# Query, key and value of a graph transformer by 26 block products instead of 3 x 7, with the token sums on GpSimd

## The chip, the cores and the metric

The kernel runs on one core of one Trainium2 chip. The metric is the device time of the whole kernel in microseconds, inputs and output in HBM, everything in fp32.

## What is computed

128 graphs of 128 nodes with 512 features each pass through two layers. The reference, cut to what matters here:

```python
# layer 0: x (128, 128, 512), adj (128, 128, 128), 8 heads of 64
h = relu(layernorm(x))
q, k, v = (h @ W.T + b for (W, b) in ((Wq, bq), (Wk, bk), (Wv, bv)))   # W: 512 x 512
scores = einsum('bhqd,bhkd->bhqk', q, k) * 64 ** -0.5 * (adj + adj)
x = x + (softmax(scores) @ v) @ Wo.T + bo
# layer 1
h = relu(layernorm(x))
Wh = h @ W
e = leaky_relu(Wh @ a[:512] + (Wh @ a[512:]).T)
att = softmax(where(adj > 0.5, e, -9e15), axis=1)
x = x + elu(att @ Wh)
```

The three products of `h` with Wq, Wk and Wv are what the change is about.

## The kernel before, in words

A *pair* `p` is two graphs (N = 64 pairs), a *group* `g` is two pairs: 4 graphs, 512 rows of `h`. 32 groups are worked through; Q, K and V are made a group at a time, everything else a pair or a graph at a time.

**Hidden rows.** `hAs[g]` holds the transposed `h` of a group: features on the partitions, in four blocks of 128 features by two pairs of 256 rows. The rows arrive transposed from HBM (`load_xT`). `hidden(p, 0)` (L222, VectorE) subtracts the mean and `hidden(p, 1)` (L224, VectorE) applies relu and scale; the numbers of a row come through HBM (`spread0` on GpSimd's DMA queue, `fetch0` on SyncE's).

**Products.** Each of Q, K and V is a 512 x 512 by 512 x 512 product, cut 2 x 2 by 2 x 2 in blocks of 256 and done with 7 block products instead of 8 (`PRODUCTS`, L130; Strassen's scheme in Winograd's form). One block product is `product` (L238): four matmul statements of 256 columns at L258. Its left operands need sums of row blocks: `token_sum` (L148 to L157) makes four per group on VectorE (`hidden_sum`, tile `hS`). Sums of weight blocks are made once at the start (`weight_sum`). The results gather in three PSUM accumulators for each of Q, K and V, `acc_a`, `acc_b` and `acc_c`. `acc_a` is read out while it still gathers: `first` copies its state into `qT`, `kT` or `v` on ScalarE (L270 for v, L275 with the bias), and `add` adds `acc_b` or `acc_c` on top on VectorE (L279).

**The rest of a pair.** `scores` (L320) makes `sc` per graph; VectorE weighs it with the adjacency (L327), takes maxima, ScalarE exponentiates and normalises, VectorE transposes 32 x 32 blocks, and two DMAs through HBM place them. `context` (L388) gives `pc` in PSUM; `keep_context` (L395) copies it to `cxT`. The output product with Wo and the later one with layer 1's W use the same seven-product scheme by rows: four token sums (`cs`, on `cxT`; `gs`, on `gT`), then `product_rows` (L299), whose accumulators `row_a` and `row_c` are added into `x` (L402) or copied and added into `z` (L495, L499). `shift` (L234, VectorE) adds a constant row to `x`. Layer 1's gather is L481 (`pg`), its dots L425, its ends `finish_a` and `finish_b` (L511, L515).

**PSUM.** One pool, `ps1` (L57), of eight buffers of 2 KB per partition serves every matmul output.

**The order.** The program states the order of all instructions by hand. `HEAD` (L577) lists steps with their pair, `ORDER` (L601) one repetition with a lag for each step, `TAIL` (L611) the end. `ORDER` is run once for each pair. Each engine takes its instructions from that list in order; between engines only data and buffers make them wait. In the names of steps, `U1` to `U11` are products, `F` and `A` their read-outs, `sca`, `scb` the scores of a pair's two graphs, `pca`, `pcb` their contexts, `o0` to `o6` and `w0` to `w6` the row products, `cs`, `gs` and `hs` the token sums, `hd0` and `hd1` the two halves of `hidden`, `sh` the shift, `lx`, `lT`, `l0` loads.

Of the kernel before, what the change touches and what calls it, by code (L numbers as in the profile page):

```python
# [10 lines left out]
OP = mybir.AluOpType  # L11
# [13 lines left out]
def kernel(  # L25
# [6 lines left out]
    wqT: bass.AP,  # L32
    bq: bass.AP,
    wkT: bass.AP,
    bk: bass.AP,
    wvT: bass.AP,
# [23 lines left out]
    xs, x0s, adjs, adjTs, hAs, hSs = {}, {}, {}, {}, {}, {}  # L60
# [18 lines left out]
    def half_of_hidden(p):  # L79

        g, i = divmod(p, 2)
        if g not in hAs:
            hAs[g] = grp.tile([P, 4, 2, 2 * S], F32, name="hA")
        return hAs[g][:, 2 * i : 2 * i + 2].rearrange("p q c k -> p (q c) k")
# [19 lines left out]
    def column(src, name):  # L104
# [10 lines left out]
    wv_sb, wq_sb, wk_sb, wo_sb, w1_sb = (  # L115
        const.tile([P, 7, 2, E // 2], F32, name=name) for name in ("wv", "wq", "wk", "wo", "w1")
    )
# [16 lines left out]
    FIRSTS = {0: (0, 0), 2: (1, 0), 4: (1, 1), 5: (0, 1)}  # L134
    ADDS = {1: (0, 0, "b"), 4: (1, 1, "c"), 6: (1, 0, "c")}
# [12 lines left out]
    def token_sum(h, s, k):  # L148

        if k == 0:  # L150
            nc.vector.tensor_tensor(s[:, 0], h[:, 2], h[:, 3], OP.add)
        elif k == 1:
            nc.vector.tensor_tensor(s[:, 1], s[:, 0], h[:, 0], OP.subtract)  # L153
        elif k == 2:
            nc.vector.tensor_tensor(s[:, 2], h[:, 0], h[:, 2], OP.subtract)
        else:
            nc.vector.tensor_tensor(h[:, 2], h[:, 1], s[:, 1], OP.subtract)  # L157
# [59 lines left out]
    def hidden(p, k):  # L217

        h = hAs[p // 2][:, 2 * (p % 2) : 2 * (p % 2) + 2].rearrange("p q c k -> p (q c) k")
        row = rows0[p][:, None, :, k].to_broadcast([P, 2 * 2, 2 * S])  # L220
        if k == 0:
            nc.vector.tensor_tensor(h, h, row, OP.subtract)  # L222
        else:
            nc.vector.scalar_tensor_tensor(h, h, 0.0, row, op0=OP.max, op1=OP.mult)  # L224

    def hidden_sum(g, k):
        if g not in hSs:
            hSs[g] = grp.tile([P, 3, 2, 2 * S], F32, name="hS")
        token_sum(hAs[g], hSs[g], k)

    def shift(p):


        nc.vector.tensor_tensor(xs[p], xs[p], c_sb[:, None, :].to_broadcast([P, 2, E]), OP.add)  # L234

    accs = {}

    def product(g, which, n):  # L238

        if n == 0:  # L240
            if which == "v":
                vs[g] = grp.tile([P, G, E], F32, name="v")
            else:
                qks[g, which] = {}
        if which != "v" and n in (0, 2):
            qks[g, which][n // 2] = grp.tile([P, C, 2 * S], F32, name=which + "T", bufs=3 if which == "q" else 2)
        w = {"q": wq_sb, "k": wk_sb, "v": wv_sb}[which]
        ha, wb, bank = PRODUCTS[n]
        fresh = (g, which, bank) not in accs
        if fresh:  # L250
            accs[g, which, bank] = ps1.tile([P, 2, 2 * S], F32, name="acc_" + bank, tag="ps1")
        acc = accs[g, which, bank]
        h = hAs[g][:, ha] if ha < 4 else hSs[g][:, ha - 4]
        for m in range(2):
            ms = slice(m * P, (m + 1) * P)
            for c in range(2):
                lhsT, rhs = (h[:, c, ms], w[:, wb, c, :]) if which == "v" else (w[:, wb, c, ms], h[:, c, :])
                nc.tensor.matmul(  # L258
                    acc[:, m, :], lhsT, rhs, start=fresh and m == 0 and c == 0, stop=c == 1, skip_group_check=True
                )  # L260

        def dst(t, f):
            if which == "v":
                return vs[g][:, 2 * t : 2 * t + 2, f * 2 * P : (f + 1) * 2 * P]
            return qks[g, which][t][:, 2 * f : 2 * f + 2, :]

        def first(t, f):
            a = accs[g, which, "a"]
            if which == "v":
                nc.scalar.copy(dst(t, f), a)  # L270
            else:
                bias = bk_sb if which == "k" else bq_sb
                for m in range(2):
                    j = 2 * f + m
                    nc.scalar.activation(dst(t, f)[:, m, :], a[:, m, :], AF.Identity, bias=bias[:, j : j + 1])  # L275

        def add(t, f, bank):
            d = dst(t, f)
            nc.vector.tensor_tensor(d, accs[g, which, bank], d, OP.add)  # L279

        def firsts():
            if n in FIRSTS:
                first(*FIRSTS[n])

        def adds():
            if n in ADDS:
                add(*ADDS[n])

        return firsts, adds
# [20 lines left out]
    def scores(b):  # L310
        p, i = divmod(b, 2)
        g, h = divmod(p, 2)
        qT, kT = qks[g, "q"][h], qks[g, "k"][h]
# [80 lines left out]
    def keep_context(b):  # L394
        nc.scalar.copy(rows_of(cxT, b % 2), pcs.pop(b))  # L395
# [88 lines left out]
    def keep_gathered(p, i):  # L484
        if p not in gTs:
            gTs[p] = work.tile([P, 7, 2, S], F32, name="gT")
        nc.scalar.copy(rows_of(gTs[p], i), pgs.pop((p, i)))  # L487
# [77 lines left out]
    SEQ = "v0 v1 v2 v3 v4 q0 v5 q1 v6 q2 q3 q4 k0 q5 k1 q6 k2 k3 k4 k5 k6".split()  # L565
# [6 lines left out]
    EARLY, LATE = 3, 4  # L572
# [197 lines left out]
    with tc.manual_schedule():  # L770
# [9 lines left out]
        for p in range(EARLY, N - LATE):  # L780
            for step, lag in ORDER:
                if p >= lag:
                    do(step, p - lag)
# [45 lines left out]
```

## Time and profile before

| | us |
|---|---|
| runs | 2347.01, 2351.15, 2352.15 |
| median | 2351.15 |
| profiled execution, first to last instruction | 2346.1 |
| TensorE busy in it | 2332.0 |
| TensorE weight loads | 2061.2 |
| VectorE busy | 2000.4 |
| ScalarE busy | 1467.2 |
| GpSimd busy | 257.0 |

The profile gives the profiled execution's span, from its first to its last instruction, and no separate time for it; the three runs lie 0.9 to 6.1 us above that span. The granted TensorE clock was 0.998 of full speed. Tables of groups name a line, an engine, an operation, `out<-in` by the program's tile names, the shape and the count; behind the bar stand busy time, mean ns of one, and the engine's idle time just before with what ended it. A fp32 matmul statement appears as two MATMUL records.

### The profile page before, as it was taken

How to read it: one execution, taken by the hardware profiler on the slowest of the kernel's cores; microseconds unless marked ns; L12 is line 12 of the kernel's file. 1: busy time of each engine (PE TensorE's matmuls, PEld its weight loads, DVE VectorE, ACT ScalarE, POOL GpSimd, SP SyncE). 2: the span in 40 equal slices, each digit the busy share in tenths (PEclk: the TensorE clock that was granted, in tenths of full speed). 3: DMA queues.
4: the chain of work that ended last, by engine and by line, in shares of the span. 5: the costliest groups of instructions: out<-in, count | busy, mean ns of one | idle time of the engine just before them, and what ended most of it. 6: DMA issues, size and time to landing. Idle time of an engine off the chain costs nothing.

```text
span 2346.1 us, 41028 instructions
## 1 busy us (share of the span) xinstructions
PE 2332.0 (99%) x14184; PEld 2061.2 (88%) x14184; DVE 2000.4 (85%) x4113; ACT 1467.2 (63%) x4815; POOL 257.0 (11%) x320
## 2 busy tenths in 40 slices
PE   9999999999999999999999999999999999999998
PEld 8888888888888888888888888888888888888886
DVE  6888888888888888888888888888888888888888
ACT  3656666666566665666666666656666566666774
POOL 1101101111101011011110111110101101110000
PEclk9999999999999999999999999999999999999999
DMA  5445454454444554544535445444454453453332
GB/s 171 131 113 157 121 147 120 124 164 125 143 131 119 148 139 130 143 114 142 155 122 149 120 123 165 124 144 131 120 148 137 131 145 108 146 153 116 118 120 95
DMA packets 267351, 314.06 MB, mean 134 GB/s; under 512 B 24200, under 2 KB 192136, under 8 KB 267144
## 3 DMA queue, kind: packets, MB, share of 16 engines
q1 hardware_dynamic: 263112, 311.31, 45.0%
q8 instruction: 112, 1.84, 0.3%
q0 software_dynamic: 1920, 0.13, 0.2%
q14 instruction: 95, 0.78, 0.1%
q10 hardware_dynamic: 2112, 0.01, 0.1%
HBM read 210.51 MB, written 100.85 MB: 133 GB/s over the span
## 4 chain that ended last, share of the span: by engine, by line
PE 99%; DVE 0%; ACT 0%; DMA 0%; issue 0%; POOL 0%; SPq 0%; ACTq 0%; DVEq 0%; POOLq 0%
PE acc_a L258 29%; PE row_a L299 24%; PE acc_c L258 14%; PE row_c L299 9%; PE acc_b L258 7%; PE sc L320 5%; PE pc L388 5%; PE pg L481 5%; PE pt L197 0%; DMA x<-in_x 0%; PE pm L531 0%; DVE st L165 0%; ACT z L495 0%; PE pu L553 0%; DVE z L499 0%
## 5 line engine op out<-in xcount | busy, mean ns | idle before, releaser
L339 ACT ACTIVATE at<-at,nmx 128x128 f32<-128x128 f32 x1024 | 396.3, 390 | 19.8 <-DVE nmx L334 17.9
L348 ACT ACTIVATE at<-at,rs 128x128 f32<-128x128 f32 x1024 | 325.0, 391 | 12.8 <-DVE rs L343 12.1
L299 PE MATMUL row_a<-wo,cxT 128*128 128x256 f32 x1280 | 328.5, 379 | 0.3 <-DVE cxT L153 0.3
L299 PE MATMUL row_a<-w,gT 128*128 128x256 f32 x1280 | 319.4, 380 | 2.9 <-DVE z L499 1.7
L172 POOL TENSOR_SCALAR mv<-mv 128x2 f32<-128x2 f32 x124 | 79.2, 639 | 2016.8 <-DVE mv L166 1994.6
L299 PEld LDWEIGHTS row_a<-w,gT 128*128 128x128 f32 x1280 | 242.3, 190 | 37.9 <-DVE z L499 2.6
L299 PEld LDWEIGHTS row_a<-wo,cxT 128*128 128x128 f32 x1280 | 242.6, 190 | 34.3 <-DVE cxT L153 0.6
L402 DVE TENSOR_TENSOR x<-row_a,x 128x256 f32<-128x256 f32 x320 | 135.3, 423 | 133.1 <-PE row_a L299 129.8
L495 ACT COPY z<-row_a 128x256 f32<-128x256 f32 x256 | 94.3, 368 | 203.7 <-PE row_a L299 203.6
L275 ACT ACTIVATE kT<-acc_a,bk 128x256 f32<-128x256 f32 x256 | 106.5, 466 | 168.2 <-PE acc_a L258 165.0
L327 DVE SCALAR_TENSOR_TENSOR at<-sc,adj 128x512 f32<-128x512 f32 x256 | 165.1, 686 | 42.2 <-PE sc L320 39.8
L339 ACT ACTIVATION_READ_ACCUMULATOR at<-at,nmx 128x1 f32 x1024 | 193.3, 189 | 0.0
L275 ACT ACTIVATE qT<-acc_a,bq 128x256 f32<-128x256 f32 x256 | 106.1, 466 | 123.0 <-PE acc_a L258 123.0
L165 DVE BATCH_NORM_STATS2 st<-x 128x6 f32<-128x512 f32 x256 | 176.1, 688 | 7.4 <-DMA x<-in_x 5.1
L425 DVE SCALAR_TENSOR_TENSOR junk<-h,u 128x512 f32<-128x512 f32 x256 | 173.3, 677 | 0.6
L355 DVE STREAM_TRANSPOSE tr<-at 128x1024 f32<-128x1024 f32 x128 | 158.8, 1240 | 9.2 <-PE pc L388 2.7
L334 DVE TENSOR_REDUCE nmx<-at 128x8 f32<-128x1024 f32 x128 | 156.2, 1220 | 4.3
L487 ACT COPY gT<-pg 128x512 f32<-128x512 f32 x128 | 74.6, 584 | 123.8 <-PE pg L481 117.4
L481 PEld LDWEIGHTS pg<-w,h 128*128 128x128 f32 x1024 | 133.3, 192 | 6.6 <-ACT z L495 0.2
L173 POOL TENSOR_TENSOR mv<-mv,mhalf 128x2 f32<-128x2 f32 x128 | 131.1, 1024 | 30.7 <-DVE mv L168 20.3
L481 PE MATMUL pg<-w,h 128*128 128x128 f32 x1024 | 134.1, 275 | 0.0
L299 PE MATMUL row_c<-w,gT 128*128 128x256 f32 x512 | 133.0, 382 | 0.6 <-DVE z L499 0.5
(130 smaller groups left out, 4876.4 us busy)
## 6 DMA issues: line engine op xcount, KB each, us to landing
blocks<-tr SPq DMA_DIRECT2D x128, 512.0 KB, 6.8
aT<-blocks SPq DMA_DIRECT2D x512, 128.0 KB, 2.9
x<-in_x SPq DMA_DIRECT2D x123, 512.0 KB, 5.0
out<-x SPq DMA_DIRECT2D x63, 512.0 KB, 4.1
hA<-in_xT SPq DMA_DIRECT2D x120, 256.0 KB, 3.7
mr<-rows SPq DMA_DIRECT2D x60, 256.0 KB, 4.4
adj<-in_adj SPq DMA_DIRECT2D x64, 128.0 KB, 4.3
adjT<-in_adjT SPq DMA_DIRECT2D x64, 128.0 KB, 4.2
```

What stands on the lines that cost most here:

```text
L165: nc.vector.bn_stats(st, src[:, i, :])
L258: nc.tensor.matmul(acc[:, m, :], lhsT, rhs, start=fresh and m == 0 and c == 0, stop=c == 1, skip_group_check=True)
L275: nc.scalar.activation(dst(t, f)[:, m, :], a[:, m, :], AF.Identity, bias=bias[:, j : j + 1])
L299: nc.tensor.matmul(acc, left[:, la, c, :], w[:, wb, c, :], start=n in (0, 3) and c == 0, stop=c == 1, skip_group_check=True)
L327: nc.vector.scalar_tensor_tensor(ats[b][0][:, k * C : (k + 1) * C, :], scs[b][k], QSCALE, adjs[p][:, i : i + 1, :].to_broadcast([P, C, S]) ...
L334: nc.vector.tensor_reduce(nmx, at, AX.X, OP.max, negate=True)
L339: nc.scalar.activation(at[:, j, :], at[:, j, :], AF.Exp, bias=nmx[:, j : j + 1], accum_out=sums[:, j : j + 1])
L348: nc.scalar.activation(at[:, j, :], at[:, j, :], AF.Copy, scale=rs[:, j : j + 1])
L355: nc.vector.transpose(trs[b], at.rearrange("p h (j k) -> p j h k", k=Q))
L402: nc.vector.tensor_tensor(d, row_acc(p, "o", bank), d, OP.add)
L425: nc.vector.scalar_tensor_tensor(junk, h2[:, i, :], 1.0, u_sb[:, k, :], op0=OP.mult, op1=OP.mult, accum_out=ws[:, i, 1:2] if k else src_sb ...
L481: nc.tensor.matmul(pg[:, c, :], h1s[p][0][:, i, c * P : (c + 1) * P], wts[p][:, i, :], start=True, stop=True)
```

## The change

Q, K and V are no longer three separate products of 2 x 2 blocks. The rows of a group are seen as 2 pairs of 256 rows, the features as 4 blocks of 128, the outputs as 4 blocks of 128: a 2 x 4 by 4 x 4 product of blocks, which takes 26 block products instead of 32. The same 26 left operands ("forms": blocks of `h` or sums of them) serve Q, K and V at once.

- `wT` holds the three weights side by side in 16 blocks; `w_sb` has 28 slots of 3 x 128 columns. 35 sums of weight slots (`block_sum`, VectorE) are made at the start instead of 12 larger ones (those of Wo and W stay).
- 17 sums of row blocks (`make_form`, GpSimd, 128 x 256 each, eight buffers `tf`) replace four 128 x 512 sums on VectorE.
- `product_qk` (2 statements of 256 columns) and `product_v` (2 statements of 128 columns) run each of 26 terms. Terms gather in 4 chains, each with an accumulator for Q and K and one for V; 24 terms are followed by a read-out (`take_qk`, `take_v`): the first one of each of the 8 output blocks on ScalarE, the 16 later ones as an add or a subtraction on VectorE.
- `hidden(p, 0)` and `shift` go from VectorE to GpSimd, each in halves of 512 elements.
- The token sums of `cxT` and `gT` read their unmixed blocks from PSUM (`pc`, `pg`) rather than from the copies that ScalarE makes. Those copies are still made.
- `HEAD`, `ORDER` and `TAIL` are new; one repetition of `ORDER` covers two pairs, and `pca`, `pcb`, `scb` follow each other while `sca` stands alone.

```diff
-        h = hAs[p // 2][:, 2 * (p % 2) : 2 * (p % 2) + 2].rearrange("p q c k -> p (q c) k")
-        row = rows0[p][:, None, :, k].to_broadcast([P, 2 * 2, 2 * S])
+        h = half_of_hidden(p)
+        row = rows0[p][:, None, :, k].to_broadcast([P, C, 2 * S])
         if k == 0:
-            nc.vector.tensor_tensor(h, h, row, OP.subtract)
+            for c in range(0, C, 2):
+                nc.gpsimd.tensor_tensor(h[:, c : c + 2], h[:, c : c + 2], row[:, c : c + 2], OP.subtract)
...
-        nc.vector.tensor_tensor(xs[p], xs[p], c_sb[:, None, :].to_broadcast([P, 2, E]), OP.add)
+        for i in range(2):
+            nc.gpsimd.tensor_tensor(xs[p][:, i, :], xs[p][:, i, :], c_sb, OP.add)
...
+    def make_form(g, k):
+
+        a, op, b = FORMS[k]
+        forms[g, 2 * C + k] = grp.tile([P, 2 * S], F32, name="tf", bufs=8)
+        eng = nc.gpsimd
+        eng.tensor_tensor(forms[g, 2 * C + k], form(g, a), form(g, b), OP.add if op == "+" else OP.subtract)
...
+    def product_qk(g, n):
+
+        _, f, slot, _ = TERMS[n]
+        acc, fresh = fresh_acc(g, n, "q", [P, 2, 2 * S])
+        for i in range(2):
+            nc.tensor.matmul(
+                acc[:, i, :], w_sb[:, slot, i, :], form(g, f), start=fresh and i == 0, stop=True, skip_group_check=True
+            )
+
+    def product_v(g, n):
+
+        _, f, slot, _ = TERMS[n]
+        acc, fresh = fresh_acc(g, n, "v", [P, 2, P])
+        for i in range(2):
+            nc.tensor.matmul(
+                acc[:, i, :], form(g, f)[:, i * P : (i + 1) * P], w_sb[:, slot, 2, :],
+                start=fresh and i == 0, stop=True, skip_group_check=True,
+            )
+
+    def take_qk(g, n):
+
+        chain, _, _, (t, j, sign) = TERMS[n]
+        acc = accs[g, chain, "q"]
...
+        d = qks[g, t][:, :, j, :]
+        if (g, t, j) not in begun:
+            begun.add((g, t, j))
+            for i, bias in enumerate((bq_sb, bk_sb)):
+                nc.scalar.activation(d[:, i, :], acc[:, i, :], AF.Identity, bias=bias[:, j : j + 1], scale=float(sign))
+        else:
+            nc.vector.tensor_tensor(d, d, acc, OP.add if sign > 0 else OP.subtract)
...
+        if (g, t, j, "v") not in begun:
+            begun.add((g, t, j, "v"))
+            nc.scalar.activation(d, acc, AF.Copy, scale=float(sign))
+        else:
+            nc.vector.tensor_tensor(d, d, acc, OP.add if sign > 0 else OP.subtract)
...
-            nc.vector.tensor_tensor(s[:, 0], h[:, 2], h[:, 3], OP.add)
+            nc.vector.tensor_tensor(s[:, 0], block(2), h[:, 3], OP.add)
...
-            nc.vector.tensor_tensor(s[:, 1], s[:, 0], h[:, 0], OP.subtract)
+            nc.vector.tensor_tensor(s[:, 1], s[:, 0], block(0), OP.subtract)
...
-            nc.vector.tensor_tensor(s[:, 2], h[:, 0], h[:, 2], OP.subtract)
+            nc.vector.tensor_tensor(s[:, 2], block(0), h[:, 2], OP.subtract)
...
-            nc.vector.tensor_tensor(h[:, 2], h[:, 1], s[:, 1], OP.subtract)
+            nc.vector.tensor_tensor(h[:, 2], block(1), s[:, 1], OP.subtract)
...
-    EARLY, LATE = 3, 4
+    EARLY, LATE = 2, 3
```

`block(q)` is a slice of the PSUM tile `pc` or `pg`. The terms that the prediction names are of `Q` (Q and K) and `V` (V) with their number in the list of 26, `T` with a number is a form's sum, `A` and `B` are the read-outs of `Q` and `V`. Around these read-outs the new `ORDER` reads, in two places:

```
... A6:0 Q13:0 Q8:0 V8:0 gs1:2 exa3:-1 A8:0 Q10:0 A11:0 T13:0 ...
... V18:0 ata1:-2 B19:0 V21:0 od4c:0 o6:0 e1:1 ez:2 sw:1 g0:1 ...
```

## The prediction

> **What bounds the kernel now.** I read the page's shares and chain first, then the timeline of TensorE at mid-run, then the groups by line and shape, then the waits. One "double pair" below means four graphs, the unit in which both kernels repeat; there are 32.
>
> ```profile
> PE 2332.0 (99%) x14184; PEld 2061.2 (88%) x14184; DVE 2000.4 (85%) x4113; ACT 1467.2 (63%) x4815; POOL 257.0 (11%) x320
> PE 99%; DVE 0%; ACT 0%; DMA 0%; issue 0%; POOL 0%; SPq 0%; ACTq 0%; DVEq 0%; POOLq 0%
> ```
>
> TensorE is busy for 99% of the span and holds all of the chain that ended last. Busy alone proves little where matmuls overlap, so the timeline (start, busy, engine, line, out<-in, count) is needed for start to start:
>
> ```profile
> 999.88 1.05 PE L481 MATMUL pg<-w,h 128*128 128x128 f32 x8
> 1000.77 1.89 PE L258 MATMUL acc_c<-hS,wq 128*128 128x256 f32 x8
> 1002.50 1.05 PE L481 MATMUL pg<-w,h 128*128 128x128 f32 x8
> 1003.49 2.06 PE L320 MATMUL sc<-kT,qT 64*128 64x128 f32 x32
> 1005.47 1.97 PE L388 MATMUL pc<-aT,v 128*64 128x128 f32 x32
> 1007.37 1.99 PE L258 MATMUL acc_a<-hS,wq 128*128 128x256 f32 x8
> 1009.20 1.03 PE L299 MATMUL row_a<-w,gT 128*128 128x256 f32 x4
> ...
> 1072.10 1.05 PE L481 MATMUL pg<-w,h 128*128 128x128 f32 x8
> ```
>
> There is no hole: each block starts where the next one's distance says. A matmul statement shows as two records. Eight records of 256 columns take 1002.50-1000.77 = 1.73 us, 0.216 each; eight of 128 columns take 1000.77-999.88 = 0.89, 0.111 each, with a new weight load for every one. A turn between full tiles and the half tiles of sc or pc costs about 0.1 us: pg before sc takes 0.99 and not 0.89, and the first full block after pc 1.83 and not 1.73. The same step comes back at 1072.10, so a double pair takes 72.2 us.
>
> The stretch from 100 to 800 us (PE, PEld, DVE, ACT, POOL busy) has TensorE at 100% and VectorE at 86%, which is 600.11/700 x 72.2 = 61.9 us of each double pair, 10.3 us free:
>
> ```profile
> 100.00:800.00 700.00, 700.00 (x4284) 620.13 (x4283) 600.11 (x1232) 442.90 (x1455) 79.00 (x97) 1.00 0.46 134
> ```
>
> The prices, from the groups by line and shape (busy and mean ns of one behind the bar, then idle time before them):
>
> ```profile
> L279 DVE TENSOR_TENSOR qT<-acc_c,qT 128x512 f32<-128x512 f32 x64 | 43.7, 683 | 4.8 <-PE acc_c L258 4.8
> L499 DVE TENSOR_TENSOR z<-row_c,z 128x256 f32<-128x256 f32 x128 | 53.0, 414 | 1.0 <-ACT z L495 0.8 <-PE row_c L299 0.2
> L222 DVE TENSOR_TENSOR hA<-hA,mr 128x1024 f32<-128x1024 f32 x60 | 72.9, 1216 | 0.0
> L234 DVE TENSOR_TENSOR x<-x,c 128x1024 f32<-128x1024 f32 x64 | 78.2, 1221 | 53.7 <-DMA x<-in_x 53.6
> L172 POOL TENSOR_SCALAR mv<-mv 128x2 f32<-128x2 f32 x124 | 79.2, 639 | 2016.8 <-DVE mv L166 1994.6
> ```
>
> ```profile
> 21.11 0.68 DVE L153 TENSOR_TENSOR hS<-hS,hA 128x512 f32<-128x512 f32 x1
> 21.72 0.68 DVE L155 TENSOR_TENSOR hS<-hA 128x512 f32<-128x512 f32 x1
> ```
>
> The second fence is VectorE's timeline at the start. Two operations of 0.68 start 0.61 apart, so each occupies the engine some 0.07 us less than its duration. VectorE's own waits, from the list of waits, are mostly for TensorE:
>
> ```profile
> DVE x L402 <- PE row_a L299: 129.8, 137, 2.0
> DVE at L327 <- PE sc L320: 39.8, 60, 1.2
> ```
>
> That is 169.6/32 = 5.3 us per double pair which VectorE can afford today.
>
> **What the Trainium skill says.** "TensorE: Matmul & The Clock Gate", Back-to-back issue gap, gives 134 cycles for 128 columns and 262 for 256, but warns that with a weight load per matmul the spacing at 128 columns grows. The trace's 0.111 against 0.216 shows the halving and no weight-load limit. "GPSIMD Engine Reference", 3.1, gives 4497 ns for a two-input fp32 add of 2048 elements and says that the engine is about half as fast as VectorE; nothing in this trace shows such an add. "SBUF — State Buffer", Who interferes with whom, says that a VectorE instruction with two SBUF inputs and a GpSimd instruction that reads SBUF lock each other out for a whole instruction; the trace before has no GpSimd work on which to see it.
>
> **The change, part by part.**
>
> *Products.* Removed: 3 x 7 products of 4 statements, 168 records of 256 columns, 168 x 0.216 = 36.3 us per double pair. Added: 26 terms with 2 statements of 256 columns (Q, K) and 2 of 128 (V): 104 x 0.216 + 104 x 0.1115 = 22.5 + 11.6 = 34.1. Gain 2.2 us on the path. At worst a V block of four pays a little more than a pg block of eight; if each of 26 lost 0.03 us, that is 0.8 back. I take 0.
>
> *Turns.* The new order runs scb behind pca and pcb, but sca alone among full tiles. Per pair that makes five turns and two returns to full tiles where there were three turns and one return: 7 x 0.095 against 4 x 0.095, +0.28 per pair, +0.57 per double pair. Net TensorE: -1.65, so 70.55 us if nothing makes it wait. Over 32: -53 us.
>
> *VectorE.* Removed per double pair: four sums hS and hA (4 x 0.685 = 2.74), nine adds of L279 (6.13), L222 twice (2.43), L234 twice (2.44): 13.74 us in 17 instructions. Added: of 26 terms 24 are read out, 8 of them first (ScalarE) and 16 later, each later one as a 128x512 add for Q and K (0.683, like L279) and a 128x256 add for V (0.415, like L499): 10.93 + 6.64 = 17.57 us in 32 instructions. Net +3.83, less 15 x 0.07 of overlap: +2.8. Busy 64.7 of 70.55, 92%, 5.9 free where 10.3 were. The token sums of cxT and gT read PSUM instead of SBUF; L402 and L499 read PSUM at 0.41-0.42 and the SBUF sums take 0.40-0.42, so 0. They no longer wait for ScalarE's copy (0.7 us in all today), but pc and pg stay in their PSUM buffers until VectorE is done.
>
> *ScalarE.* 16 Q and K evictions stay 16 at 0.466; four V copies of 512 (0.583) become eight of 256 (0.368): +0.6 us on an engine at 63%. Off the path: nothing.
>
> *GpSimd.* Added: 17 sums of 256 elements, four halves of the subtraction and four of the shift at 512. By the skill's 2.2 ns an element (an estimate) 17 x 0.56 + 8 x 1.12 = 18.5 us; with L172's 0.64 us for two elements as a fixed cost on each of the 25, 34.5. With the 8.1 us it has (79.00/700 x 72.2) it is 27 to 43 us of 70: not a bound by load. But row statistics (L172, L173) now queue behind sums, and behind a subtraction that waits for its DMA. Most sums are issued 5 to 69 us of TensorE work ahead of their first product; T16, T12 and T6 only 1.8, 3.1 and 5.2.
>
> *The lock.* 18 VectorE instructions per double pair have two SBUF inputs (scaling of hidden 2, dots 8, the finish 4, mask and shares 4). If GpSimd reads for 18.5 of 70.55 us (26%) and a hit waits half an instruction, 0.4 us, that is 18 x 0.26 x 0.4 = 1.9 us. From below 0 (no lock), from above 5 (the long GpSimd durations). I take 2: VectorE 66.7 of 70.55, 95%.
>
> *Waits that are left.* A term's next product into the same accumulator waits for the read-out of the one before. In the new order Q10 stands 0.45 us of TensorE work behind Q8, whose read-out is two ScalarE instructions of 0.47, and V21 1.3 us behind V19 with 1.5 us of VectorE work queued between. Others have 1.7 to 20 us. With 3.9 us free on VectorE and 5.3 us of its waits to fit in, I take 0.5 us of new TensorE waits per double pair: +16 us. Lower bound 0; the upper one is rival 1.
>
> *Start and end.* 35 sums of weight blocks (128x384, about 0.49 us each, between L499's and L279's cost) stand where 12 of 0.61 stood: 17.2 - 7.3 = +10 us of VectorE before the products run freely. The first Q product needs a sum of the second pair's hidden rows, the first one now needs the first pair's alone and starts at 11.4 us. Part of this was idle TensorE already: +6, between 0 and 15. The end keeps its steps: 0. SP issues 4 weight DMAs where 6 were: nothing.
>
> *Sum.* 2346.1 - 53 + 6 + 16 = 2315 us of span. The median of the runs shown lies 5 us above the span: 2320.
>
> **Rivals.**
> 1. *VectorE becomes the bound: slower.* Its 64.7 us, 2.8 us of lock, and waits for TensorE as long as today's 5.3 make 72.8; with 0.2 for read-outs held up behind the statistics, 73.0. Over 32 that is +0.8 x 32 = 26, start +6: 2346 + 32 + 5 = 2383. It decides once lock plus waits exceed 72.2 - 64.7 = 7.5 us. For it: the sum of today's waits and the lock is within half a microsecond of that. Against: most of today's waits are spare time of an engine at 86% and shrink as it fills.
> 2. *The gain is eaten by latency.* GpSimd sums arriving late (three of them with under 5.3 us in hand) or PSUM: four chains hold two accumulators each, four of eight buffers at any time, and pc and pg hold theirs longer. Waits of 1.4 us per double pair: 2346 - 53 + 6 + 45 + 5 = 2349, no change. Against: GpSimd at 27-43 of 70 us has room.
> 3. *No new wait and no dearer start.* 2346 - 53 + 5 = 2298. Against: today's evenness rests on 10 us of free VectorE.
>
> **How the numbers follow.** Forecast 0.62 (2298 to 2340), rival 1 0.20, rival 2 0.13, rival 3 0.05. About 0.2% either way, 2346 to 2356, is what a measurement can tell from no change. Rival 2 straddles it: 0.04 below, 0.06 in, 0.03 above. So faster 0.71, same 0.06, slower 0.23. The range 2290 to 2378 leaves out half of rival 1 and little below.
>
> **What would show it.** Right: blocks of 128-column acc_v at 0.11 us a record, a double pair of 70.5 to 71.5 us, TensorE at 98%, VectorE near 94%. Rival 1: VectorE above 96% and TensorE waiting for its acc_q and acc_v adds in steady state; two-SBUF-input groups (L425's 677 ns and the finish's 1.2 us) grown by 10% or more. Rival 2: TensorE waiting for tf sums, or for buffers of pc and pg. The start is wrong if the first 60 us hold over 20 us of idle TensorE. A GpSimd sum of 256 elements over 1.3 us would break the load sum.

## The result, and the profile after

| us | before | after |
|---|---|---|
| median of the runs | 2351.64 (2347.01 to 2352.15) | 2471.76 (2470.09 to 2476.72) |
| span of the profiled execution | 2346.1 | 2470.0 |
| TensorE busy | 2332.0 | 2334.7 |
| VectorE busy | 2000.4 | 2175.2 |
| GpSimd busy | 257.0 | 987.1 |
| one double pair, mean over the middle of the run | 72.2 | 75.76 |

The change makes the kernel slower: the ratio of the medians is 1.052, with a 95% interval of 1.050 to 1.053. The forecast of 2320 is missed by 152 us and lies on the other side of the kernel before. (The median of before is now of four runs; the table ahead of the prediction had three.)

The page of after, shares and chain:

```profile
PE 2334.7 (95%) x15464; PEld 2038.7 (83%) x15464; DVE 2175.2 (88%) x4620; ACT 1470.0 (60%) x4943; POOL 987.1 (40%) x1112
PE 72%; DVE 14%; DMA 7%; issue 3%; SPq 2%; ACT 2%; POOL 0%; DVEq 0%; POOLq 0%; ACTq 0%
```

No engine is full. TensorE holds 72% of the chain where it held 99%, and the rest is VectorE and transfers. GpSimd, the engine with the new work, has no part in it. The stretch from 100 to 800 us (columns as before) says how much TensorE lacks:

```profile
100.00:800.00 700.00, 670.67 (x4483) 587.57 (x4483) 623.88 (x1336) 424.83 (x1440) 289.12 (x327) 1.00 0.44 127
```

A TensorE that shows as busy is not always at work: 670.67/700 x 75.76 = 72.6 us busy per double pair stand for 70.9 us of blocks (worked out below, step by step). The timeline of TensorE shows such a lack, and that its own prices are as forecast:

```profile
1038.19 1.03 PE L297 MATMUL acc_q<-hA,w 128*128 128x256 f32 x4
1039.05 1.03 PE L346 MATMUL row_a<-wo,cxT 128*128 128x256 f32 x4
1039.92 0.61 PE L306 MATMUL acc_v<-w,hA 128*128 128x128 f32 x4
1040.36 1.03 PE L297 MATMUL acc_q<-hA,w 128*128 128x256 f32 x4
1042.89 0.68 PE L306 MATMUL acc_v<-w,tf 128*128 128x128 f32 x4 [1.50 <-ACT v L334]
1043.41 1.03 PE L346 MATMUL row_c<-wo,cxT 128*128 128x256 f32 x4
```

Four records of 256 columns take 1039.92-1039.05 = 0.87 us, four of 128 columns 1040.36-1039.92 = 0.44. Then `V6` starts 2.53 us behind its predecessor, which needed 0.87: 1.7 us are lost to a ScalarE copy of `v` (`B4`). Why the copy was late is in VectorE's timeline of the same moment, of which these lines count (behind the bracket, idle time and what ended it), and in ScalarE's:

```profile
1037.08 0.42 DVE L449 TENSOR_TENSOR x<-row_a,x 128x256 f32<-128x256 f32 x1
1040.12 0.42 DVE L449 TENSOR_TENSOR x<-row_a,x 128x256 f32<-128x256 f32 x1 [2.61 <-PE row_a L346]
1040.46 0.68 DVE L205 BATCH_NORM_STATS2 st<-x 128x6 f32<-128x512 f32 x1
...
1041.59 0.17 DVE L390 RECIPROCAL rs<-sums 128x4 f32<-128x4 f32 x1
```

```profile
1041.79 0.69 ACT L395 ACTIVATE at<-at,rs 128x128 f32<-128x128 f32 x2 [2.08 <-DVE rs L390]
1042.39 0.36 ACT L334 ACTIVATE v<-acc_v 128x256 f32<-128x256 f32 x1
```

VectorE stands 2.61 us at `od1`, an addition of `row_a` into `x` (L449), whose tile `row_a` TensorE is still writing. Behind `od1` in VectorE's fixed queue stands, after some other work, a reciprocal of 0.17 us; for it ScalarE stands 2.08 us; behind that in ScalarE's queue stands the copy; for it TensorE stands. A wait of VectorE for TensorE has come back to TensorE through two queues.

The chain in order of time (start, us, what) shows the other end of the same wait:

```profile
1039.22 0.88 PE row_a L346 x4
...
1040.46 0.70 DVE st L205
...
1045.32 1.16 DVE tr L402
1046.50 3.97 DMA blocks<-tr
...
1053.77 1.16 DVE nmr L459
...
1060.39 1.65 DVE junk L472 x2
1062.03 0.35 DVE gT L197
1062.52 1.10 PE row_a L346 x4
```

From 1040 to 1062 us VectorE works with a single pause of 0.16 us, and at the end TensorE waits for a token sum. That this is what had piled up behind the wait is a reading of the chain. The groups by line and shape give the prices (columns as before):

```profile
L323 DVE TENSOR_TENSOR qk<-qk,acc_q 128x512 f32<-128x512 f32 x512 | 335.1, 671 | 7.2 <-PE acc_q L297 4.4
L336 DVE TENSOR_TENSOR v<-v,acc_v 128x256 f32<-128x256 f32 x512 | 208.2, 408 | 40.3 <-PE acc_v L306 37.4
L282 POOL TENSOR_TENSOR tf<-hA,tf 128x256 f32<-128x256 f32 x288 | 259.4, 905 | 386.4 <-PE acc_v L306 260.6 <-PE acc_q L297 124.6
L472 DVE SCALAR_TENSOR_TENSOR junk<-h,u 128x512 f32<-128x512 f32 x256 | 229.5, 896 | 6.3 <-ACT h L465 2.7
L263 POOL TENSOR_TENSOR hA<-hA,mr 128x512 f32<-128x512 f32 x120 | 191.7, 1617 | 70.3 <-DMA hA<-in_xT 59.5 <-PE sc L367 6.7 <-issue 2.5
L459 DVE SCALAR_TENSOR_TENSOR nmr<-mv 128x2 f32<-128x2 f32 x64 | 38.9, 608 | 0.2 <-POOL mv L213 0.2
```

The read-outs cost what was forecast (0.683 and 0.415 were taken). The dots have grown from 677 to 896 ns, and an operation of two columns (L459) from 155 to 608. The list of waits (us in all, times, longest):

```profile
ACT at L386 <- DVE nmx L381: 198.2, 118, 5.4
DVE x L449 <- PE row_a L346: 149.6, 94, 2.6
ACT at L395 <- DVE rs L390: 78.0, 63, 3.3
PEld acc_v L306 <- POOL tf L282: 41.9, 23, 1.9
PE acc_v L306 <- ACT v L334: 41.2, 28, 1.5
PE acc_q L297 <- ACT qk L321: 16.5, 34, 0.9
```

In the kernel before ScalarE waited 17.9 us in the place of the first line and 12.1 in that of the third. VectorE's wait for `row_a` hasn't shrunk with VectorE's free time: 149.6 us now, 129.8 before. The fourth line, weight loads for V that wait for a GpSimd sum, looks like rival 2, but belongs to the copy of the line below it: the sum that `V6` reads, `T5`, is made a repetition earlier (`T5:-2`), and in e2_dead below, where nobody waits for GpSimd, the same loads wait 57.2 us for the copy.

### The profile page after: what moved, and what is told of

It is laid out like the page before. It is cut to its first block, busy times and chain, and to the rows that moved or that the text cites. A ratio compares the mean times of both kernels' runs of the same rounds, so it can differ in the third digit from the quotient of the medians.

```text
span 2470.0 us, 45694 instructions
## 1 busy us (share of the span) xinstructions
PE 2334.7 (95%) x15464; PEld 2038.7 (83%) x15464; DVE 2175.2 (88%) x4620; ACT 1470.0 (60%) x4943; POOL 987.1 (40%) x1112
## 4 chain that ended last, share of the span: by engine, by line
PE 72%; DVE 14%; DMA 7%; issue 3%; SPq 2%; ACT 2%; POOL 0%; DVEq 0%; POOLq 0%; ACTq 0%
PE acc_q L297 20%; PE row_a L346 18%; PE acc_v L306 12%; PE row_c L346 8%; PE sc L367 5%; PE pc L435 4%; DMA aT<-blocks 4%; PE pg L528 4%; DVE junk L472 3%; SPq L412 2%; DMA blocks<-tr 2%; DVE qk L323 1%; DVE hA L265 1%; DVE st L205 1%; DVE x L449 1%
## 5 line engine op out<-in xcount | busy, mean ns | idle before, releaser
L297 PE MATMUL acc_q<-tf,w 128*128 128x256 f32 x2176 | 556.3, 383 | 17.7 <-ACT qk L321 15.9
L297 PEld LDWEIGHTS acc_q<-tf,w 128*128 128x128 f32 x2176 | 393.1, 190 | 76.7 <-ACT qk L321 23.3
L282 POOL TENSOR_TENSOR tf<-hA,tf 128x256 f32<-128x256 f32 x288 | 259.4, 905 | 386.4 <-PE acc_v L306 260.6
L306 PEld LDWEIGHTS acc_v<-w,tf 128*128 128x128 f32 x2176 | 312.3, 191 | 89.4 <-POOL tf L282 41.9
L306 PE MATMUL acc_v<-w,tf 128*128 128x128 f32 x2176 | 334.0, 279 | 42.9 <-ACT v L334 40.5
L323 DVE TENSOR_TENSOR qk<-qk,acc_q 128x512 f32<-128x512 f32 x512 | 335.1, 671 | 7.2 <-PE acc_q L297 4.4
L297 PE MATMUL acc_q<-hA,w 128*128 128x256 f32 x1152 | 291.0, 380 | 0.8 <-ACT qk L321 0.6
L449 DVE TENSOR_TENSOR x<-row_a,x 128x256 f32<-128x256 f32 x320 | 134.1, 419 | 151.0 <-PE row_a L346 149.6
L336 DVE TENSOR_TENSOR v<-v,acc_v 128x256 f32<-128x256 f32 x512 | 208.2, 408 | 40.3 <-PE acc_v L306 37.4
L297 PEld LDWEIGHTS acc_q<-hA,w 128*128 128x128 f32 x1152 | 211.2, 190 | 26.5 <-ACT qk L321 1.3
L263 POOL TENSOR_TENSOR hA<-hA,mr 128x512 f32<-128x512 f32 x120 | 191.7, 1617 | 70.3 <-DMA hA<-in_xT 59.5
```

Source lines behind the costliest of these rows:

```text
L263: nc.gpsimd.tensor_tensor(h[:, c : c + 2], h[:, c : c + 2], row[:, c : c + 2], OP.subtract)
L282: eng.tensor_tensor(forms[g, 2 * C + k], form(g, a), form(g, b), OP.add if op == "+" else OP.subtract)
L297: nc.tensor.matmul(acc[:, i, :], w_sb[:, slot, i, :], form(g, f), start=fresh and i == 0, stop=True, skip_group_check=True)
L306: nc.tensor.matmul(acc[:, i, :], form(g, f)[:, i * P : (i + 1) * P], w_sb[:, slot, 2, :], start=fresh and i == 0, stop=True, skip_group_ch ...
L323: nc.vector.tensor_tensor(d, d, acc, OP.add if sign > 0 else OP.subtract)
L336: nc.vector.tensor_tensor(d, d, acc, OP.add if sign > 0 else OP.subtract)
```

## The experiments

Four theories. *Load*: VectorE's work, grown by 2.8 us and by the lock, with its waits in between, is the bound (the forecast's rival 1). *Lock*: it is GpSimd's hold on VectorE. *Latency*: sums from GpSimd, PSUM buffers or the transfer of the attention come late (rival 2). *Order*: the parts cost what was forecast, but in this sequence of steps the waits of three in-order queues feed each other. In the expectations of the first four runs "order" still takes VectorE's load in; the two were separated after them. "Double pair" times are means over the middle of each run; TensorE's own need is some 70.9 us, so the rest of each is waiting.

**GpSimd's work: left out, done for nobody, done without reading.** e1_none leaves the additions out, e2_dead does them on a private tile, e3_fill replaces each by three constant fills of the same tile, with all waits kept; each does the same with the halves of `hidden(p, 0)` and `shift`.

```diff
 e1_none
-        eng.tensor_tensor(forms[g, 2 * C + k], form(g, a), form(g, b), OP.add if op == "+" else OP.subtract)
+        forms[g, 2 * C + k] = hAs[g][:, source(k)]
 e2_dead, in addition
+        nc.gpsimd.tensor_tensor(dead[:, 0, 0 : 2 * S], dead[:, 1, 0 : 2 * S], dead[:, 2, 0 : 2 * S], OP.add)
 e3_fill
-        eng.tensor_tensor(forms[g, 2 * C + k], form(g, a), form(g, b), OP.add if op == "+" else OP.subtract)
+        for _ in range(3):
+            nc.gpsimd.memset(forms[g, 2 * C + k], 0.5)
```

Expected of e1_none: 

> Leaves out the 25 GpSimd additions per double pair (the 17 sums of row blocks, the subtraction of the mean and the shift by the constant row): the products read a plain block of the hidden rows in place of a sum. TensorE, ScalarE and VectorE keep all their instructions and the order stays. Theories: (lock) GpSimd's reads hold up VectorE's instructions with two SBUF inputs by about 3.5 us per double pair, and TensorE pays for that; (late) TensorE pays because the GpSimd results themselves arrive late; (order) the VectorE load of 65 us per double pair and the read-outs between the terms are what TensorE waits for, whatever GpSimd does. Lock and late: 2310 us, between 2290 and 2340, a double pair of 70.5 to 71.5 us. Order: 2430 or more.

Expected of e2_dead: 

> As e1_none, but GpSimd executes the same 25 additions per double pair, of the same sizes and at the same places of its queue, on a private tile that nobody else reads or writes. The results are left out of the computation as in e1_none. Nobody can wait for them; only their reads of SBUF are left. Lock: 2400 to 2470 us, with the dots (junk) again near 0.9 us. Late: as e1_none, 2310 to 2330. Order: as e1_none, over 2430.

Expected of e3_fill: 

> The changed kernel, but each GpSimd addition is replaced by three fills of its output tile with a constant, of about the same total length (three of 512 elements for 1.4 to 1.6 us, three of 256 for 0.8 us): GpSimd writes the same tiles, the others wait for them as before, but it reads no SBUF. What the additions compute is left out. Lock: 2310 to 2340 us, the dots at 0.68 us. Late: 2430 to 2470. Order: 2430 or more.

Measured: 2430.48, 2467.89 and 2435.57. The same additions cost as much when nobody waits for their results (4 us less than after), and fills on which everybody waits cost only 5 us more than nothing, so GpSimd's sums are not late. Fills take 36 us less than the additions, with GpSimd about as busy, so most of the 41 us between after and e1_none lies in what GpSimd's reading does to VectorE. In e3_fill the two groups are back at their old size:

```profile
L474 DVE SCALAR_TENSOR_TENSOR junk<-h,u 128x512 f32<-128x512 f32 x256 | 175.5, 686 | 6.2 <-ACT h L467 2.6
L461 DVE SCALAR_TENSOR_TENSOR nmr<-mv 128x2 f32<-128x2 f32 x64 | 9.1, 143 | 0.2 <-POOL mv L213 0.2
```

(The lines of these two stand two lower in that kernel.) The Trainium skill, "SBUF — State Buffer", Who interferes with whom, has a VectorE instruction with two SBUF inputs contend with a GpSimd instruction that reads SBUF, and not with one that only writes it; the runs agree: 896 ns beside a GpSimd that reads, 686 beside one that only writes. But without any GpSimd addition 78 us of slowdown are left, and a double pair takes 74.38. The lock is a third of the loss in this order, not the whole of it.

**The two long operations back on VectorE, and the other way round.** e4_long_back takes `hidden(p, 0)` and `shift` of after back to VectorE as 128x1024; e6_before_long moves them to GpSimd in the kernel before.

```diff
 e4_long_back (e6_before_long: the reverse, in the kernel before)
-            for c in range(0, C, 2):
-                nc.gpsimd.tensor_tensor(h[:, c : c + 2], h[:, c : c + 2], row[:, c : c + 2], OP.subtract)
+            nc.vector.tensor_tensor(h, h, row, OP.subtract)
...
-        for i in range(2):
-            nc.gpsimd.tensor_tensor(xs[p][:, i, :], xs[p][:, i, :], c_sb, OP.add)
+        nc.vector.tensor_tensor(xs[p], xs[p], c_sb[:, None, :].to_broadcast([P, 2, E]), OP.add)
```

Expected of e4_long_back: 

> Undoes one part: the subtraction of the mean and the shift go back to VectorE as single instructions of 1024 elements (1.2 us each, four per double pair, +4.6 us of VectorE), the 17 sums stay on GpSimd. VectorE's plain load is then about 69.5 us per double pair against TensorE's 70.5. Lock: the long reads of 1.4 to 1.6 us are gone, so the dots fall back to 0.75 us or less, but VectorE has no room left: 2400 to 2480 us. Order: VectorE's load decides, so clearly slower than the changed kernel, over 2500. Late: 2440 to 2480.

Expected of e6_before_long: 

> The kernel before with one part of the change alone: the subtraction of the mean and the shift on GpSimd in halves of 512 elements, in the old order. VectorE loses 4.9 us per double pair and has some 14 us free. GpSimd's reads will lock some of VectorE's two-input instructions (dots above 0.72 us on average). If the lock costs only where VectorE has no room: 2345 to 2356 us, no change. If the moved steps come late (the shift is read by the first output sums): 2370 or more.

Measured: 2559.67 and 2354.04. In the order of after, 4.9 us more of VectorE's instructions per double pair (four of 1.22) cost 88 us, 2.6 per double pair, although GpSimd and with it the lock have less. In the order of before, moving it to GpSimd changes the time by 0.1% (0.0 to 0.2). The lock is there too. It hits the token sums, which read SBUF alone in that kernel, and hardly the dots (696 ns, under the 0.72 us expected); first before, then e6_before_long:

```profile
L151 DVE TENSOR_TENSOR cxT<-cxT 128x256 f32<-128x256 f32 x64 | 26.8, 418 | 0.4 <-ACT cxT L395 0.4
```

```profile
L151 DVE TENSOR_TENSOR cxT<-cxT 128x256 f32<-128x256 f32 x64 | 58.6, 916 | 0.0
```

Four such groups have grown by 92 us, 2.9 per double pair, as much as the lock takes in after. An order with room feels neither the relief nor the lock.

**Load, tried from both sides.** e10_short_dots takes 4.5 us per double pair of VectorE's work out of after at unchanged places ((2175.2 - 2031.1)/32, by the busy times); e12_before_load puts 5.2 us more into the kernel before ((2165.7 - 2000.4)/32).

```diff
 e10_short_dots
-            junk, h2[:, i, :], 1.0, u_sb[:, k, :], op0=OP.mult, op1=OP.mult, accum_out=...
+            junk[:, 0:2], h2[:, i, 0:2], 1.0, u_sb[:, k, 0:2], op0=OP.mult, op1=OP.mult, accum_out=...
 e12_before_load
             nc.vector.tensor_tensor(d, accs[g, which, bank], d, OP.add)
+            junk = work.tile([P, E], F32, name="junk")
+            nc.vector.tensor_tensor(junk, u_sb[:, 0, :], u_sb[:, 1, :], OP.add)
```

Expected of e10_short_dots: 

> The kernel after with the eight dot products of a double pair cut to 2 of 512 elements (layer 1's scores are those of two features only): some 5.5 us plus their share of the lock less on VectorE, at the same places of its queue, and none of it is work that the change touched. VectorE theory: the period falls by about as much as VectorE's work, to the 70.6 us of TensorE plus what is left, 2320 to 2390 in all. Latency theory: the transfers stay, 2440 to 2472.

Expected of e12_before_load: 

> The kernel before with nine more VectorE adds of 128x512 per double pair, on a tile that nobody waits for, one behind each read-out of L279: 5.6 us more, VectorE at 93 to 94 per cent instead of 86. If VectorE's filling alone makes TensorE wait: 30 to 110 us slower. If the old order has the room: within 10 us of 2352.

Measured: 2435.67 and 2380.68. The stretch from 100 to 800 us, of e10_short_dots and then of e12_before_load:

```profile
100.00:800.00 700.00, 677.90 (x4531) 596.57 (x4530) 586.18 (x1352) 428.56 (x1455) 284.72 (x332) 1.00 0.46 130
```

```profile
100.00:800.00 700.00, 692.93 (x4187) 611.24 (x4187) 643.33 (x1306) 436.62 (x1428) 75.08 (x93) 1.00 0.48 132
```

With VectorE at 586.18/700 = 84%, less than in the kernel before, the order of after still leaves TensorE idle for 22 of 700 us (74.46 per double pair). With VectorE at 92%, more than in after, the order of before leaves 7. Load does cost: e10_short_dots, between its two expectations, gained 36 us for 144 taken out (some of it lock), and e12_before_load, at the lower edge of "30 to 110 us slower", lost 29 for 165 put in, 0.18 us for each. But it doesn't make the difference. The load theory falls.

**Latency of the transfer, and the PSUM reads.** e9_no_trip lets the context products read the transposed blocks directly; e11_copies lets the token sums read ScalarE's copies, as before.

```diff
 e9_no_trip (send_blocks and place_blocks)
-        nc.sync.dma_start(blocks[b].rearrange(...), trs.pop(b).rearrange("p j h k -> p (j h k)"))
+        blocks[b] = trs.pop(b)
...
+        aTs[b] = blocks.pop(b)
 e11_copies
-            return bank(q // 2)[:, q % 2 * 2 : q % 2 * 2 + 2, :]
+            return h[:, q]
```

Expected of e9_no_trip: 

> The kernel after without the way of the transposed attention through HBM: the context products read the 32x32 blocks as VectorE left them (the output's attention is therefore wrongly placed); five DMAs per graph and some 8 us between the flip and the context are gone, all VectorE work stays. Latency theory (the ring flip, two transfers, context, row products, flip sets the period): 2300 to 2380. VectorE theory (its own queue, with the waits for row_a in it, sets the period): 2440 to 2472.

Expected of e11_copies: 

> One part of the change undone: the sums of context and gathered blocks read ScalarE's copies, as before. If PSUM buffers that pc and pg hold longer make TensorE wait: 20 us or more faster, below 2452. If it only trades a wait for ScalarE against one for PSUM: within 10 us of 2472, or up to 20 slower because eight sums of a double pair now wait for the copies.

Measured: 2460.14 and 2535.92. Five transfers per graph and the 8 us that they take, gone from the chain, give 12 us. Undoing the PSUM reads costs 64, more than expected. Two causes are mixed in that: the sums wait for the copies again, and with two inputs in SBUF they meet the lock. In its trace the sum of L193 on `gT` takes 780 ns where it took 414, and the eight groups of sums together 68 us more of VectorE. How the 64 us divide was not measured; what is shown is that this order can't do without the PSUM reads. Nothing of latency explains 120 us.

**Moving what visibly waits.** e5_readouts puts `B4` and `Q10` where TensorE needn't wait for them, e7_place moves two placements of the attention forward, e8_both does both.

```diff
 e5_readouts (Q10 likewise, to right behind w2:2)
-        ... Q4:0 od4c:1 rcb1:0 nmb3:0 lT:-1 hd0:-1 B4:0 V6:0 A7:0 ...
+        ... Q7:0 pr:2 exb3:0 B4:0 nmb0:0 fa:3 ...
```

In e7_place `pla:0` stands right behind `blb:0`, and `pla:-1` right behind `rca0:-2`.

Expected of e5_readouts: 

> The changed kernel with two steps of its repetition moved: B4 (the read-out of V's term 4 on ScalarE) from behind two normalisations that wait for VectorE's reciprocal to a place before them, and Q10 from directly behind the read-out A8 it waits for to three product steps later. In the changed kernel's trace TensorE stands 1.7 us at V6 (which waits for B4) and 0.75 us at Q10 in every double pair. Order as the cause, each stall by itself: 2.4 us less in each of some 28 double pairs, 2405 us, between 2395 and 2425. If these waits only hide a later one (VectorE's load): 2440 to 2475.

Expected of e7_place: 

> The changed kernel with the first graph's loads of the turned attention blocks (pla) moved up in SyncE's queue for both pairs: from just before the context products that use them to just behind the blocks' sending, and ahead of plb. In the trace the context products wait 0.7 us in one pair and up to 1.6 us with other waits in the other. If the late issue of these loads is what they wait for: 2440 to 2455 us. If they wait for PSUM buffers that VectorE frees late: within 5 us of 2472.

Expected of e8_both: 

> The moves of e5_readouts and e7_place together. Independent stalls: the gains add, 2375 to 2400 us. One chain behind all of them: no more than the better of the two.

Measured: 2502.40, 2504.25 and 2529.73, all slower than after, by 30 to 58 us. In e5_readouts TensorE's waits for `v` and `qk` are all but gone, but its weight loads wait 45.5 us for the normalised attention ahead of `pg` and 36 us for a sum ahead of `row_a`. The expectations that a removed wait is a gain fall: here the place where TensorE is seen waiting is not the place where the delay begins. What e7_place delays was not followed.

**Moving where the delay begins.** e13_od1 moves the one step at which VectorE waited 2.61 us. `od1` reads the half of `row_a` that `o1` wrote, but stood behind `o5`, which writes the other half of the same tile, and so waited for `o5`.

```diff
-        sh:1 cs2:1 cs3:1 A3:0 exb0:0 V2:0 od0:1 T8:0 wd6:3 wm:2 ...
+        sh:1 cs2:1 cs3:1 A3:0 exb0:0 V2:0 od0:1 od1:1 T8:0 wd6:3 wm:2 ...
...
-        ... nmb0:0 fa:3 od4:1 o5:1 nmb1:0 od1:1 t0:-2 V7:0
+        ... nmb0:0 fa:3 od4:1 o5:1 nmb1:0 t0:-2 V7:0
```

Expected: 

> The kernel after with one step moved: od1 of one pair, the add that reads row_a where VectorE waits for TensorE's o5 although o5 writes the other half of that tile, stands right behind od0, before o2. Order theory (a wait for TensorE inside VectorE's fixed queue holds up what TensorE needs next): 15 to 35 us faster than after, 2437 to 2457, and the wait of x for row_a shrinks. If it is only one of several rings of equal length: within 10 us of 2472.

Measured: 2417.38, ratio to before 1.028 (1.0265 to 1.030), 54 us faster than after, which is more than expected and more than all of GpSimd's work left out had given. In its list of waits

```profile
DVE x L449 <- PE row_a L346: 80.3, 67, 2.1
ACT at L395 <- DVE rs L390: 22.1, 38, 3.3
```

VectorE's wait for `row_a` is down from 149.6, ScalarE's for the reciprocal from 78.0, and TensorE's for the copy of `v`, 41.2 in after, is no longer in the list, nor is that of the weight loads for `tf`. The lock is a little smaller as well (the dots take 836 ns), some 0.8 us of VectorE's time per double pair, so not all of the 54 us need be the stall. The other wait named above, `Q10` for its read-out, is there as in after (16.5).

**The whole sequence.** e14_new_order has the same 341 steps per repetition, each with its lag, in another sequence: on the mean a step stands 6 places from where it stood, at most 52. Among the moves are `od1:1` (ahead of `o5:1`, as in e13_od1), `hd0:-1` (13 places earlier, ahead of `od1:1`) and `V6:0`:

```diff
-        ... o5:1 nmb1:0 od1:1 t0:-2 V7:0 Q4:0 od4c:1 rcb1:0 nmb3:0 lT:-1 hd0:-1 B4:0 V6:0 A7:0 ...
+        ... nmb0:0 nmb1:0 Q7:0 T11:0 hd0:-1 cs3:1 fa:3 l0:-2 t0:-2 od4:1 od4c:1 V4:0 od1:1 exb2:0 rcb1:0 la:-1 Q4:0 B4:0 ... e1:2 o5:1 od5:1 nmb2:0 f0:0 B7:0 T6:0 sw:2 o6:1 od6:1 V6:0 fb:3 ...
```

Expected of e14_new_order: 

> The kernel after with the same 341 steps in each repetition of the order, none added or removed, but standing in another sequence within the repetition (read-outs, adds and sums moved by up to 40 places; start and end unchanged). Order theory: the parts cost what the forecast said and TensorE's own 70.6 us set the period, 70.6 to 71.4 us, in all 2320 to 2350. Load theory (VectorE's 67.5 us of work and lock and its waits for TensorE are the bound whatever the order): not below 2430. Latency of GpSimd's sums or of PSUM as the bound: not below 2430 either.

Expected of e15_new_order_none (the same sequence without GpSimd's additions, edit as in e1_none): 

> The same other sequence with the 25 GpSimd additions of a double pair left out (the products read plain blocks, hidden isn't centred, the shift is missing). If the lock costs something by itself: 20 to 40 us faster than with them, as it was in the order of after. If it costs only where the order has no room: within 8 us of the run with them.

Measured: e14_new_order 2354.78, 117 us below after and 0.16% above before (0.07 to 0.25). Its page and its stretch from 100 to 800 us:

```profile
PE 2314.4 (98%) x15464; PEld 2033.7 (86%) x15464; DVE 2115.8 (90%) x4620; ACT 1458.3 (62%) x4943; POOL 922.7 (39%) x1112
PE 92%; DVE 3%; DMA 2%; ACT 1%; SPq 1%; issue 1%; POOL 0%; POOLq 0%; DVEq 0%; ACTq 0%
```

```profile
100.00:800.00 700.00, 698.23 (x4681) 615.59 (x4681) 636.39 (x1400) 445.61 (x1521) 285.74 (x345) 1.00 0.46 136
```

With the same instructions TensorE is busy for 698 of 700 us beside a VectorE at 91%, and a double pair takes 71.44 us. This sequence also keeps GpSimd's additions and VectorE's dots apart: the dots take 708 ns instead of 896. That can't be the main part of the gain, since no GpSimd work at all left 2430 in the old sequence. The clean comparison is with e1_none: VectorE is busy for 605.63/700 x 74.38 = 64.4 us of a double pair there and 636.39/700 x 71.44 = 64.9 here, and yet the double pair is 2.9 us shorter. That is the sequence alone.

e15_new_order_none missed both expectations: 2381.94, 27 us slower than e14_new_order with less work. VectorE now waits 74 us for loads of `x` and TensorE 34 us for the adds into `x`. Such a sequence suits one set of times; which of the missing waits lets the load come late was not followed. So the cost of the lock in this sequence was not measured; in that of before e6_before_long had found none.

**The ends.** e16_new_ends puts `HEAD` and `TAIL` into another sequence too and moves the steps of the repetition again (by 4.5 places on the mean, at most 39); e17_ends_of_e14 keeps the repetition of e14_new_order and changes only the ends in that manner. No step is added or removed.

Expected of e16_new_ends: 

> The sequence of e14 with the lists of the start and of the end put into another sequence too (same steps, same dependences; some steps of the repetition moved again by a few places). In e14 TensorE's last 100 us hold 19.9 us without a matmul and the first 100 us 14.1, against 8.8 and 5.2 in the kernel before. If that is what separates e14 from the forecast: 5 to 20 us faster than e14, 2335 to 2350, below the kernel before. If not the ends: within 4 us of 2355.

Expected of e17_ends_of_e14: 

> The repetition of e14, unchanged, with the start and the end in a sequence as in e16. In e16 the last 100 us held 3.4 us more of TensorE's work than in e14 and the first 100 us 1.2 more, while its repetition, with the half tiles apart from each other in more places, took 71.9 us instead of 71.4. If both readings hold: 4 to 12 us faster than e14, 2343 to 2351, and below the kernel before. If the repetition was not what made e16 slower: at 2365 again.

Measured: e16_new_ends 2365.45, slower than e14_new_order although its ends are shorter, because its repetition takes 71.89 us. The reason given for that in the second expectation is wrong: both sequences have eight turns between full and half tiles per double pair. The 0.45 us are waiting (1.1 us per double pair against 0.6, by the sum of the next section), spread over many blocks; VectorE is busy for 66.4 us there against 64.9. Why was not found. e17_ends_of_e14 2345.09, ratio to before 0.9973 (0.9963 to 0.9983): the fastest of all, 127 us below after and 0.27% below before. Its period is 71.43, its first 100 us hold 88.8 us of TensorE's work and its last 86.2; in after these were 85.9 and 80.5, in before 94.8 and 91.2.

## Why the prediction was wrong, step by step

- *Products, turns.* Held, but for 0.3 us. The records lie 0.216 and 0.111 us apart as taken. TensorE's need can be summed from its timeline between 200 and 2160 us, with each block at the distance that it keeps where nothing is waited for (16 records of `sc` or `pc` take 1.09 or 1.03 us, and 0.1 goes on either side of such half tiles). The sum gives 72.15 of 72.2 us in the kernel before, and 70.9 in after, e13_od1 and e14_new_order alike, where 70.55 was worked out. The turns are the term that was too small.
- *VectorE +2.8.* Held in its terms: 0.671 and 0.408 for read-outs taken at 0.683 and 0.415. In e3_fill, without the lock, VectorE is busy for 604.79/700 of 74.72 us, 64.6 against the 64.7 forecast.
- *GpSimd.* Held: 0.73 to 0.91 us for 256 elements and 1.43 to 1.62 for 512, inside the bounds of 0.56 to 1.2 and 1.12 to 1.75; 40% busy; its results are not late (e2_dead). The price of the Trainium skill, "GPSIMD Engine Reference", 3.1, from which I took 2.2 ns an element as an estimate, is too low here: 2.8 to 3.5 ns, waits for the lock among them.
- *The lock.* Right in kind, too small in size: 1.9 us were worked out. Of VectorE's 67.5 us in after (623.88/700 x 75.76) 64.6 are without it, so it took 2.9. The operation of two columns (L459) was not among the 18 counted and makes (38.9 - 9.1)/32 = 0.9 of it: even two columns wait for a GpSimd addition, 608 against 155 ns. The forecast took the PSUM reads at 0; that they keep the token sums out of the lock (e6_before_long, e11_copies) it didn't see.
- *Waits that are left, 0.5 us.* This is the step that failed. A double pair waits 75.76 - 70.9 = 4.9 us where 0.5 was taken. I looked for read-outs that stand close behind their product, found `Q10` (which waits 16.5 us in all) and took the rest from VectorE's mean free time. The largest wait comes from a chain through three queues instead: VectorE stands at a step for TensorE, and what stands behind it is needed by ScalarE and TensorE. Nothing of that was in the counted distances. The sequence decides it: in e14_new_order the same sum leaves 0.6 us of waiting, the size that was forecast. I had the line for it: VectorE's 129.8 us of waits for `row_a` before, read as "time that VectorE can afford". It can afford them only where nothing urgent is queued behind.
- *Rival 1* has the right sign and names VectorE's waits, which stay (4.7 us per double pair for `row_a` alone, where 4.1 were before) instead of shrinking. Its reason, VectorE as the bound, is refuted by e10_short_dots, e12_before_load and e14_new_order. *Rival 2* is refuted by e2_dead and e3_fill for the sums and by e9_no_trip for the transfers; for PSUM by e14_new_order, which has the same eight buffers and the same tiles to put in them. That a new order may itself cost what the parts save was not among the rivals at all.
- *Start +6, end 0.* TensorE's first 100 us hold 8.9 us less work than before (85.92 against 94.82) and its last 100 us 10.7 less (80.49 against 91.15). These are busy times, and the clock granted in the first 100 us was 0.93 in after and 0.97 before, so the work missing at the start can be up to 4 us more. The end was taken as unchanged because its steps are; its sequence is not.

The sum with measured terms, over the some 29.5 double pairs between the ends: 2346.1 + 29.5 x (75.76 - 72.2) + 8.9 + 10.7 = 2471, against a span of 2470.0. With e17_ends_of_e14's 71.43, start of +6.1 and end of +5.0 it gives 2334, against 2343.3 measured. The missing 9 us lie in the start and the end: between the 13th and the 113th transposition of attention blocks (L355 in before, L402 here) this kernel is 21 us faster than before, up to there 10.5 us slower and from there on 8. The clock granted in its first 100 us was 0.91 against 0.97, which can account for up to 6.

How the 4.9 us divide, by the same sum over the blocks: 1.8 are lost between products of Q, K and of V, nearly all of it ahead of `V6`; 1.4 between the context products of two graphs; 0.7 ahead of products of Q and K that follow one of V, `Q10` among them; the rest in small pieces. In e13_od1 the 1.8 are gone and 2.8 in all are left (75.76 to 73.70), so this part hangs on one step. What holds the context products up is not settled: the list puts their waits down to several engines, and in e14_new_order they are gone.

## What to carry to other kernels

Where all engines run a sequence that is written down, a change of the sequence is a cost of its own: price it by asking, for each place where an engine waits for the bound engine, what is queued behind that wait and who needs it within the next few microseconds. When the bound engine waits, follow the chain back through the queues to the first engine that stood still, and move that step; moving the last link only handed the wait on here. This rests on one such chain in one kernel. A mean share tells little: VectorE at 91% held next to nothing up in one sequence, and at 84%, with less work, TensorE still stood idle in another.

## What the runs showed of the hardware that was not expected

- A VectorE operation of 128x2 with two SBUF inputs takes 0.61 us on average beside GpSimd additions (1.24 us at 1053.70 us of after, beside two additions of 128x512), 0.14 beside GpSimd fills.
- Token sums of 128x256 on VectorE took up to 0.92 us beside GpSimd additions where both inputs lay in SBUF (e6_before_long), and 0.41 to 0.42 where one lay in PSUM (after).
- GpSimd's fills, at about the same share of busy time, lengthen neither the dots (686 ns) nor the operation of two columns (143 ns).
- The lock need not cost time: 2.9 us of it per double pair, with 4.9 us of VectorE's work moved away, left the time within 0.2% in one order (e6_before_long), while in another GpSimd's additions cost 41 us (after against e1_none).
